# Softmax inverses and two late weights moved to GpSimd's DMA queue, in a two-layer attention kernel

## The chip, the cores and the metric

The kernel runs on one core of one Trainium2 chip. The metric is the device time of one execution in microseconds, taken as the median of several runs. Everything is float32.

## What is computed

The reference applies two layers to an image batch `x` of shape (8, 32, 32, 512).

```
# layer 0: group norm, 8-head self-attention over 1024 tokens, residual
xn  = group_norm(x) * gn_scale + gn_bias                 # 32 groups of 16 channels
qkv = xn @ w_qkv + b_qkv
out = softmax(q k^T / 64) v                              # per image, 8 heads of 64
x   = x + out @ w_out + b_out

# layer 1: deformable attention over 256 sampled keys, per image
q_img   = layernorm(x) @ wq + bq
o       = gelu(depthwise_conv_7x7_stride2(q_img) + dw_b)
offsets = tanh(o @ pw_w)                                 # 16 x 16 points
smp     = bilinear_samples(x, reference_points + offsets)
kv      = smp @ wv + bv
att     = softmax((x @ mq_w + mq_b)(kv @ mk_w + mk_b)^T) (kv @ mv_w + mv_b)
z       = att @ mo_w + mo_b + x
out     = gelu(layernorm(z) @ mlp_w + mlp_b) + z
```

## The kernel before

The kernel makes two passes. The **first pass** (about 0 to 2130 us) is layer 0, with the depthwise convolution of the images that are already done woven into it. The **second pass** is the rest of layer 1. The instructions of every engine run in the order in which the program issues them (`InOrder`), so each engine, and each engine's DMA queue, is a strict line. All of the pass's instructions are issued through one helper, which is why the profile puts nearly all of them on line 54.

The first pass is a row of 256 **units**. A unit is one tile of 128 queries for one pair of heads; an image has 4 pairs times 8 tiles, 32 units (`per`). In a unit, `MovedAttention.push` (lines 206 to 220)

- has TensorE compute two tiles of scores `sc` (one for each head, 128 by 1024),
- has VectorE take their negated maxima `nmax`, and ScalarE the exponentials `e` with their row sums,
- has VectorE transpose `e` in blocks of 32 into `sq`.

After every second unit, `moved` (lines 222 to 231) issues 16 DMAs `et<-sq` of 128 KB on SyncE's queue, which complete the transpose. TensorE multiplies `et` by the values about two units later (`part`, tile `av`). A **block** is four units: four query tiles of one head pair, which share one `av` tile.

When a block's four tiles of sums are complete, `share` (lines 170 to 180) has VectorE take their reciprocals and transpose them into `rsT`; a DMA stores `rsT` in DRAM as `rs_d`. `spread` (lines 182 to 191) reads it back with two DMAs `inv<-rs_d`, each of which hands one head's inverses to 64 partitions. `scale` (line 193) multiplies `av` by `inv` into `attT`.

All other work is put into **places**. `at(place, step)` notes a step for a place counted in units; `run_due` runs the noted steps in order of place, those below n + 0.8 between the exponentials and the transposes of unit n, and those below n + 1 after them. So a place decides where in each engine's line a step's instructions stand. The places that the change and the prediction touch are these:

- `attention_out` (lines 767 to 785): for a block whose last unit is m, n = m + 3. `share` is at n - 1.9, `spread` at n - 1.1 (for the last three blocks of the pass n - 0.3), the scaling at n + 1.85. SyncE's queue carries the store and both reads; for the last three blocks it is GpSimd's queue.
- `conv_chunk` (lines 919 to 966): the depthwise convolution runs in units 26 to 56 of the plan, by taps. For one kind of tap ScalarE multiplies into one of two buffers `part_x` and GpSimd adds it to `oa`; the other kind VectorE does alone. A unit's taps stand at 0.05 and 0.9.
- `out_steps` (lines 708 to 765): for each of an image's 8 output tiles GpSimd fetches `xr`, adds a bias row, and later multiplies and adds the normalized tile `hat`; SyncE's queue stores `mid` (the residual sum) and `hat_d`. The convolution's operand comes from `hat_d`.
- `load_weight` (line 540): GpSimd's queue loads a whole weight (1 MB) into the single tile `w`: `w_out` at 0.95 and 9.95, `wq` at 7.6 and 15.6 of an image.
- `fold_steps` (lines 800 to 878): in the last image, weights of layer 1 are multiplied with one another beforehand. It loads `wv` (at 17.7) and `mk_w` (19.3) whole by GpSimd; `w_out` (25.2 and on, four quarters, 0.5 units apart) and `mv_w` (27.2 and on, four quarters, 0.7 apart) come by ScalarE's queue. Tile `raw` shares its three buffers with the normalized input `xT`.

The second pass calls `share` and `spread` too, on SyncE's queue (lines 1401 and 1405).

Of the kernel before, what the change touches and what calls it, by code (L numbers as in the profile page):

```python
# [9 lines left out]
F32 = mybir.dt.float32  # L10
# [7 lines left out]
P = 128  # L18
B = 8
H = W = 32  # L20
S = H * W
C = 512
NC = C // P
NT = S // P
# [42 lines left out]
class Attention:  # L67
# [99 lines left out]
                    stop=(j == nkt - 1),  # L167
                )

    def share(self, sums, queue=None):  # L170

        nc = self.nc
        self.queue = queue or nc.sync
        rs = self.shares[self.turns % 2]
        self.turns += 1
        nc.vector.reciprocal(rs[:, 0 : 2 * NQT], sums.rearrange("p h i -> p (h i)"))
        turned = self.work.tile([P, SQ], F32, tag="rsT", name="rsT", bufs=2)
        nc.vector.transpose(turned, rs)
        self.share_d = self.dram.tile([P, SQ], F32, tag="rs_d", name="rs_d", bufs=3)
        self.queue.dma_start(self.share_d, turned)  # L180

    def spread(self):

        inv = self.work.tile([P, NSQ, NQT, SQ], F32, tag="inv", name="inv", bufs=self.n_inv)
        there = self.share_d.rearrange("(r c) q -> r (c q)", r=NSQ)
        for h in range(2):
            self.queue.dma_start(
                inv[ds(h * HD, HD)].rearrange("p r i q -> p r (i q)"),
                there[:, ts(h, NQT * SQ)].partition_broadcast(HD),
            )  # L190
        return inv
# [57 lines left out]
def attention_then_deformable_attention(  # L249
# [30 lines left out]
    nc = tc.nc  # L280
# [20 lines left out]
    def by_chunk(w):  # L301
        return w.rearrange("(c p) o -> p c o", p=P)
# [65 lines left out]
    def at(place, step):  # L368
        due.append((place, len(due), step))
# [140 lines left out]
    with ExitStack() as l0:  # L510
# [3 lines left out]
        nc = InOrder(tc)  # L514
# [23 lines left out]
        room_w = {}  # L538
# [3 lines left out]
            room_w["w"] = work.tile([P, NC, C], F32, tag="w", name="w", bufs=1)  # L542
            nc.gpsimd.dma_start(room_w["w"], by_chunk(w))

        def load_quarter(w, c):
            if c == 0:
                room_w["w"] = work.tile([P, NC, C], F32, tag="w", name="w", bufs=1)
            nc.scalar.dma_start(room_w["w"][:, c, :], by_chunk(w)[:, c, :])

        lng_row = load_row(wp, ln_g, "lng_row")  # L550
        lnb_row = load_row(wp, ln_b, "lnb_row")

# [214 lines left out]
        def attention_out(attT, hp, qt, n, et, sums, values):  # L767

            blk, t = divmod(qt, NQT)
            half = t // 2  # L770
            for first in (True, False):
                at(n + 1.02 - first, lambda first=first: att.part(et, values, hp, half, first))
            if half == 0:
                return

            share = {}

            def scale():
                t = attT[hp, blk] = work.tile([P, QB], F32, tag="attT", name="attT", bufs=NQB * NHP)
                att.scale(t, share["inv"])  # L780

            last = n > B * per - NT
            at(n - 1.9, lambda: att.share(sums, nc.gpsimd if last else nc.sync))
            at(n - (0.3 if last else 1.1), lambda: share.update(inv=att.spread()))
            at(n + 1.85, scale)

        def last_places(n, t):
# [12 lines left out]
        def fold_steps(first):  # L800

            raws, wT = {}, {}

            rows = {}

            def row(name, dst, raw, vec):
                rows[name] = ByRow(dst, raws[raw], vec)

            def spare():
                return work.tile([P, NC, QB], F32, tag="xT", name="raw", bufs=NX_T)  # L810

            def fetch(name, w):
                raws[name] = spare()
                nc.gpsimd.dma_start(raws[name], by_chunk(w))

            def turn(name, m):
                if name == "v" and m == 0:
                    wT[name] = spare()
                src = room_w["w"] if name == "v" else raws["wq"]
                ps = mm_tile()  # L820
                for c in range(NC):
                    nc.tensor.transpose(ps[:, ts(c, P)], src[:, c, ts(m, P)], ident)
                nc.scalar.copy(wT[name][:, m, :], ps)

            def product(dst, tag, name, raw, i):
                if i == 0:
                    fold[dst] = kept(tag)
                ps = project(lambda m: wT[name][:, m, ts(i, P)], lambda m: raws[raw][:, m, :])
                nc.scalar.copy(fold[dst][:, i, :], ps)

            at(first + 18.3, number)
            for part in range(4):
                at(first + 18.35 + part, lambda part=part: load_biases(part))
            at(first + 19.3, set_refs)
            at(first + 17.7, lambda: load_weight(wv))
            at(first + 19.3, lambda: fetch("mk", mk_w))
            for m in range(NC):
                at(first + 23.5 + m // 2 + 0.05 * (m % 2), lambda m=m: turn("v", m))
            def quarter(name, w, c):
                if c == 0:  # L840
                    raws[name] = spare()
                nc.scalar.dma_start(raws[name][:, c, :], by_chunk(w)[:, c, :])

            for c in range(NC):
                at(first + 25.2 + 0.5 * c, lambda c=c: load_quarter(w_out, c))
                at(first + 27.2 + 0.7 * c, lambda c=c: quarter("mv", mv_w, c))
                at(first + per + 1.24 + 0.001 * c, lambda c=c: quarter("wq", wq, c))
            for i, place in enumerate((25.5, 27.5, 28.5, 29.5)):
                at(first + place, lambda i=i: product("wvk", "wC", "v", "mk", i))
            def row_tile():  # L850
                return work.tile([P, C], F32, tag="v", name="row_b", bufs=5)

            def col_tile():
                return work.tile([P, NC], F32, tag="mu", name="col", bufs=2)

            at(first + 24.65, lambda: row("k", bvk, "mk", bv_c))
            at(first + 24.651, lambda: rows["k"].away(row_tile(), nc.gpsimd))
            at(first + 27.9, lambda: rows["k"].back(col_tile(), nc.gpsimd))
            raws["wq"] = None

            for i, place in enumerate((30.5, 31.5, 32.5, 32.52)):
                at(first + place, lambda i=i: product("wvv", "wB", "v", "mv", i))
            last = first + per
            at(last + 0.6, lambda: wT.update(q=spare()))
            at(last + 2.41, lambda: rows["k"].add(nc.vector))
            at(last + 3.5, lambda: row("v", bvv, "mv", bv_c))
            at(last + 3.51, lambda: rows["v"].away(row_tile(), nc.scalar))
            at(last + 4.28, lambda: rows["v"].back(col_tile(), nc.scalar))
            at(last + 3.6, lambda: fetch("mq", mq_w))
            for m in range(NC):  # L870
                at(last + 4.27 + 0.001 * m, lambda m=m: turn("q", m))
            for i in range(NC):
                at(last + 4.5 + 0.01 * i, lambda i=i: product("wqq", "wA", "q", "mq", i))
            at(last + 4.48, lambda: row("q", bqq, "mq", bq_c))
            at(last + 4.481, lambda: rows["q"].away(row_tile(), nc.scalar))
            at(last + 4.515, lambda: rows["q"].back(col_tile(), nc.scalar))
            for name in ("v", "q"):
                at(last + 4.9, lambda name=name: rows[name].add(nc.vector))
# [208 lines left out]
    with ExitStack() as l1:  # L1087
# [297 lines left out]
        def unit_steps(n):  # L1385
            hi, hp = divmod(n, NHP)
            b = hi // 2
            u = dict(tiles=NQT, at=0, v=lambda j, h: vals[b][:, j, ds((2 * hp + h) * HD, HD)])

            def scores():  # L1390
                u["q"], u["k"] = queries.pop((hi, hp)), keys[b][:, hp, :]
                u["e"] = att.scores(u)

            def scale():
                if hp == 0:
                    attH[hi] = work.tile([P, NHP, QB], F32, tag="attH", name="attH")
                att.scale(attH[hi][:, hp, :], u["inv"])

            at(n, scores)
            at(n + 0.02, lambda: att.moved(u, 0))  # L1400
            at(n + 0.039, lambda: att.share(u["sums"]))
            at(n + 0.04, lambda: att.moved(u, 1))
            at(n + 0.0401, lambda: att.taken(u, 0))
            at(n + 0.041, lambda: att.taken(u, 1))
            at(n + 0.0411, lambda: u.update(inv=att.spread()))
            last = n + 1 == 2 * B * NHP
            at(n + (1.3 if last else 1.1), lambda: att.product(u))
            at(n + (1.305 if last else 1.2), scale)
            if not last and n:
                at(n + 0.042, lambda: query_step(*divmod(n + 1, NHP)))  # L1410
# [135 lines left out]
```

## Time and profile before

| what | value |
|---|---|
| median of 3 runs | 3262.32 us (3259.76 to 3265.22) |
| the profiled execution | 3264.03 us, span 3262.3 us |
| mean granted TensorE clock | 0.998 |
| instructions | 59564 |
| data moved by DMA | 674.31 MB, mean 207 GB/s |
| DMA time, share of 16 engines: SyncE's queue (q1) | 56.8% |
| the same: GpSimd's (q0) | 13.7% |
| the same: ScalarE's (q10) | 0.4% |

The profile comes from one execution. Times are counted from the first instruction of the span. PE is TensorE's matmul, PEld its weight load, DVE is VectorE, ACT is ScalarE, POOL is GpSimd, SP is SyncE; a q behind a name means the engine's instruction queue. A row of a waits view reads: who waited, for whom, in total, how often, the longest. A row of a timeline reads: start, duration, engine, operation, and in brackets the idle time before it and what ended it. The page leaves out instructions that issue DMAs when it counts busy time.

### The profile page before, as it was taken

The page shows a single profiled execution, that of the slowest core. Times are in us where ns is not written, and L with a number is a line of the kernel's source. Part 1 is how long each engine was busy: PE and PEld are TensorE (multiplying, and loading weights), DVE is VectorE, ACT ScalarE, POOL GpSimd, SP SyncE. Part 2 cuts the span into 40 slices and gives each one's busy share as a digit, 9 for nine tenths or more (in the row PEclk, how much of TensorE's full clock was granted, in tenths as well). Part 3 has the DMA queues.
Part 4 walks back from the last instruction along what each step waited for, and adds up shares of the span by engine and source line. Part 5 has one row for each costly group of instructions (what it writes and reads, how often), then busy time and mean ns, then how long its engine had stood idle before and what let it go on. Part 6 is the DMA issues. An engine that isn't in the chain of part 4 may idle for free.

```text
span 3262.3 us, 59564 instructions
## 1 busy us (share of the span) xinstructions
PE 3217.9 (99%) x21588; PEld 1301.2 (40%) x21588; DVE 2522.9 (77%) x3457; ACT 1780.8 (55%) x3826; POOL 1593.5 (49%) x2026
## 2 busy tenths in 40 slices
PE   8999999999999999999999999999999999999999
PEld 4444344344344444444444434333333333333333
DVE  5776778898888888788788888557868787676765
ACT  3443356566567567557657656335555555554442
POOL 1001316755764665664674577225556565653323
PEclk9999999999999999999999999999999999999999
DMA  5666766777677766676676677678777786887873
GB/s 171 169 179 162 210 181 180 211 200 186 204 196 191 203 197 177 204 211 178 181 223 183 177 216 211 180 228 272 219 240 242 228 264 211 264 259 229 265 236 130
DMA packets 479325, 674.31 MB, mean 207 GB/s; under 512 B 76828, under 2 KB 268632, under 8 KB 478776
## 3 DMA queue, kind: packets, MB, share of 16 engines
q1 hardware_dynamic: 434528, 529.53, 56.8%
q0 software_dynamic: 41136, 136.78, 13.7%
q10 hardware_dynamic: 3368, 4.20, 0.4%
q8 instruction: 171, 2.80, 0.4%
q14 instruction: 122, 1.00, 0.1%
HBM read 263.17 MB, written 138.69 MB: 123 GB/s over the span
## 4 chain that ended last, share of the span: by engine, by line
PE 89%; DVE 3%; ACT 2%; DMA 2%; POOL 1%; issue 1%; SPq 1%; POOLq 0%; DVEq 0%; ACTq 0%
PE mm L54 55%; PE sc L54 17%; PE av L54 17%; ACT e L54 1%; DVE nmax L54 1%; SPq L54 1%; DMA et<-sq_d 1%; DVE sq L54 1%; POOL oa L54 0%; DVE chunk L54 0%; DMA w<-in_L_conv_w_out_dram 0%; DMA sq_d<-sq 0%; POOL xr L54 0%; DMA row<-mid,ii 0%; ACT part_x L54 0%
## 5 line engine op out<-in xcount | busy, mean ns | idle before, releaser
L54 ACT ACTIVATE e<-sc,nmax 128x1024 f32<-128x1024 f32 (+1 forms) x1024 | 803.0, 797 | 531.4 <-DVE nmax L54 524.7
L54 DVE TENSOR_REDUCE nmax<-sc 128x1 f32<-128x1024 f32 (+1 forms) x640 | 750.2, 1212 | 291.3 <-PE sc L54 286.0
L54 POOL TENSOR_TENSOR oa<-part_x,oa 128x256 f32<-128x256 f32 x852 | 639.4, 751 | 542.5 <-ACT part_x L54 496.4
L54 DVE STREAM_TRANSPOSE sq<-e 128x1024 f32<-128x1024 f32 x640 | 764.3, 1225 | 118.5 <-ACT e L54 97.7
L54 ACT ACTIVATE part_x<-pad_x,dww_x 128x256 f32<-128x256 f32 x852 | 441.2, 545 | 259.9 <-POOL oa L54 258.4
L54 PE MATMUL sc<-k,q 64*64 64x512 f32 x4096 | 512.3, 603 | 8.8 <-ACT e L54 6.7
L54 PE MATMUL av<-et,v 128*64 128x256 f32 x4096 | 499.2, 386 | 11.7 <-DMA et<-sq 4.5
L54 PEld LDWEIGHTS av<-et,v 128*64 128x64 f32 x4096 | 273.7, 137 | 328.8 <-issue 162.1
L54 POOL TENSOR_TENSOR mv<-mv,minus_half 128x1 f32<-128x1 f32 x128 | 76.3, 596 | 389.0 <-DVE mv L54 388.0
L54 PEld LDWEIGHTS sc<-k,q 64*64 64x64 f32 x4096 | 137.5, 132 | 314.6 <-issue 208.4
L54 POOL TENSOR_TENSOR chunk<-parts,chunk 128x256 f32<-128x256 f32 x240 | 185.3, 772 | 137.2 <-ACT parts L54 123.2
L54 DVE SCALAR_TENSOR_TENSOR od<-pad_x,dww_x,od 128x256 f32<-128x256 f32 x276 | 232.7, 843 | 5.5
L54 PE MATMUL mm<-wo,attH 128*64 128x512 f32 x1024 | 233.7, 598 | 0.0
L54 PE MATMUL mm<-wC,xT 128*64 128x256 f32 x2048 | 232.1, 379 | 0.0
L54 PE MATMUL mm<-xT,wB 128*64 128x512 f32 x1024 | 230.7, 592 | 0.6 <-DVE xT L54 0.6
L54 PE MATMUL mm<-hat_h,wA 128*64 128x512 f32 x1024 | 230.9, 593 | 0.0
L54 PE MATMUL mm<-xT,wA 128*64 128x512 f32 x1024 | 230.7, 592 | 0.0
L54 PE MATMUL mm<-w,attT 128*64 128x512 f32 x1024 | 230.1, 592 | 0.3 <-DMA w<-in_L_conv_w_out_dram 0.3
L54 PE MATMUL mm<-wm,zT 128*64 128x512 f32 x976 | 220.7, 592 | 0.5 <-ACT zT L54 0.5
L54 ACT ACTIVATION_READ_ACCUMULATOR e<-sc,nmax 128x1 f32 x1024 | 209.1, 204 | 0.0
L54 PEld LDWEIGHTS mm<-wC,xT 128*64 128x64 f32 x2048 | 148.0, 137 | 77.7 <-issue 6.4
L54 PE MATMUL mm<-w,hat_x 128*64 128x512 f32 x768 | 170.2, 593 | 0.0
(198 smaller groups left out, 3457.6 us busy)
## 6 DMA issues: line engine op xcount, KB each, us to landing
et<-sq SPq DMA_DIRECT2D x2048, 128.0 KB
sq_d<-sq SPq DMA_DIRECT2D x128, 512.0 KB
et<-sq_d SPq DMA_DIRECT2D x128, 512.0 KB
inv<-rs_d SPq DMA_DIRECT2D x250, 128.0 KB
xr<-mid POOLq DMA_DIRECT2D x64, 256.0 KB
xr<-in_x_dram POOLq DMA_DIRECT2D x62, 256.0 KB
x<-in_x_dram POOLq DMA_DIRECT2D x60, 256.0 KB
out_dram<-res POOLq DMA_DIRECT2D x60, 256.0 KB
```

The lines of the kernel that those rows point to most:

```text
L54: return self.tc.keep_in_program_order(op(*args, **kwargs))
```

## The change

In the first pass, all blocks now use GpSimd's queue for the store of `rsT` and the two reads of the inverses, not just the last three. VectorE's part stays at n - 1.9. The store becomes a step of its own at n - 1.17, and the reads stand at n - 0.3 for all blocks. (For the last three blocks the queue and the reads' place are as before, and only the store moves, from n - 1.9 to n - 1.17.) In the last image, `w_out` and `mv_w` are loaded whole by GpSimd's queue at 25.2 and 27.2 instead of in quarters by ScalarE's. The quarters of `wq` at the end of the pass stay on ScalarE's queue. The second pass issues the same as before, through a step `shared`.

```diff
-    def share(self, sums, queue=None):
+    def share(self, sums):
         nc = self.nc
-        self.queue = queue or nc.sync
         rs = self.shares[self.turns % 2]
         self.turns += 1
         nc.vector.reciprocal(rs[:, 0 : 2 * NQT], sums.rearrange("p h i -> p (h i)"))
         turned = self.work.tile([P, SQ], F32, tag="rsT", name="rsT", bufs=2)
         nc.vector.transpose(turned, rs)
         self.share_d = self.dram.tile([P, SQ], F32, tag="rs_d", name="rs_d", bufs=3)
-        self.queue.dma_start(self.share_d, turned)
+        return turned
 
-    def spread(self):
+    def spread(self, queue):
...
         for h in range(2):
-            self.queue.dma_start(
+            queue.dma_start(
...
-        def load_quarter(w, c):
-            if c == 0:
-                room_w["w"] = work.tile([P, NC, C], F32, tag="w", name="w", bufs=1)
-            nc.scalar.dma_start(room_w["w"][:, c, :], by_chunk(w)[:, c, :])
...
-            last = n > B * per - NT
-            at(n - 1.9, lambda: att.share(sums, nc.gpsimd if last else nc.sync))
-            at(n - (0.3 if last else 1.1), lambda: share.update(inv=att.spread()))
+            at(n - 1.9, lambda: share.update(rs=att.share(sums)))
+            at(n - 1.17, lambda: nc.gpsimd.dma_start(att.share_d, share["rs"]))
+            at(n - 0.3, lambda: share.update(inv=att.spread(nc.gpsimd)))
             at(n + 1.85, scale)
...
+            at(first + 25.2, lambda: load_weight(w_out))
+            at(first + 27.2, lambda: fetch("mv", mv_w))
             for c in range(NC):
-                at(first + 25.2 + 0.5 * c, lambda c=c: load_quarter(w_out, c))
-                at(first + 27.2 + 0.7 * c, lambda c=c: quarter("mv", mv_w, c))
                 at(first + per + 1.24 + 0.001 * c, lambda c=c: quarter("wq", wq, c))
...
+            def shared(u):
+                rs = att.share(u["sums"])
+                nc.sync.dma_start(att.share_d, rs)
...
-            at(n + 0.039, lambda: att.share(u["sums"]))
+            at(n + 0.039, lambda: shared(u))
...
-            at(n + 0.0411, lambda: u.update(inv=att.spread()))
+            at(n + 0.0411, lambda: u.update(inv=att.spread(nc.sync)))
```

## The prediction

> **What bounds the kernel now.** I read the page's busy shares first, then what TensorE waited for, then what SyncE's queue waited for in the first pass (30 to 2100 us), and last the rows around single places.
>
> ```profile
> PE 3217.9 (99%) x21588; PEld 1301.2 (40%) x21588; DVE 2522.9 (77%) x3457; ACT 1780.8 (55%) x3826; POOL 1593.5 (49%) x2026
> ```
>
> TensorE is busy for 3217.9 of 3262.3 us, at a granted clock of 0.998. So no change of queues can win more than the 44 us that are left, and some 13 of those are the start (the first 100 us hold 87.2 us of work). What TensorE waited for, over the whole span:
>
> ```profile
> PE mm L54 <- DMA x<-in_x_dram: 8.4, 1, 8.4
> PE sc L54 <- ACT e L54: 7.7, 10, 1.3
> PE av L54 <- DMA et<-sq_d: 5.0, 4, 2.2
> PE av L54 <- DMA et<-sq: 4.5, 3, 2.5
> PE av L54 <- DVE rs L54: 2.7, 1, 2.7
> PE av L54 <- DVE mv L54: 1.6, 2, 1.1
> ```
>
> An `av` wait is one for the moved exponentials `et`. The releaser named is not always the last one: by the trace's DMA records the `DVE rs` row (at 2058) and the `DVE mv` rows (at 356 and 1927) end when the last of 16 `et` transfers lands. The same holds for a wait of 1.0 us at 878 that is put down to `DVE od`. So 1.1 us at 356, 1.0 at 421, 1.0 at 878, 0.5 at 1927, 2.5 at 1998 and 2.7 at 2058 are waits for `et`. In SyncE's queue:
>
> ```profile
> SPq L54 <- DVE sq L54: 251.5, 79, 31.4
> SPq L54 <- DMA rs_d<-rsT: 103.3, 55, 5.9
> SPq L54 <- POOL hat L54: 44.0, 27, 4.6
> SPq L54 <- DMA et<-sq: 35.1, 34, 2.9
> ...
> SPq L54 <- DMA raw<-in_L_conv_mv_w_dram: 5.5, 2, 4.6
> SPq L54 <- DMA w<-in_L_conv_w_out_dram: 4.8, 2, 4.4
> ```
>
> The reader is to see two things. The queue that carries `et` stands still for 103 us because an inverse may only be read once the sums' tile has landed. And it stands still, twice for over 4 us, for weights that it did not send: these are the quarters on ScalarE's queue.
>
> **What goes from SyncE.** 61 blocks lose one `rs_d` (median 0.57 us) and two `inv` (0.61 each): 61 x 1.79 = 109 us of issue, and the 103 us of waiting. Nearly all of it is hidden: most groups of 16 `et` land 1 to 9 us before TensorE wants them. It shows only where the wait above follows such a block:
>
> ```profile
> 402.83 0.41 SPq L54 DMA_DIRECT2D mid<-xr  x1
> 403.32 0.71 SPq L54 DMA_DIRECT2D rs_d<-rsT  x1
> 404.12 0.87 SPq L54 DMA_DIRECT2D hat_d<-hat  x1
> 407.13 1.27 SPq L54 DMA_DIRECT2D inv<-rs_d  x2
> 408.51 14.55 SPq L54 DMA_DIRECT2D et<-sq  x21
> ```
>
> These `et` could have gone at 405.74, when `sq` was written. They went 2.8 us later, and the last landed at 421.77, 0.1 us before TensorE's late start. Without `rs_d` and `inv` the queue is free at 405, so the 1.0 us goes. The groups that end at 356, 878 and 1927 began 2.9, 1.7 and 2.8 us late for the same reason: 1.1 + 1.0 + 0.5 go too. The one at 1998 began 0.9 us late and then waited 2.7 us for an `inv` to land; the load of `wv` is in its way as well (8.67 us to landing), so I take 1.5 of its 2.5. Sum: **5.1 us won**; bounds 2.5 (half of it is lost to hat rows that come later) and 6.1 (all five waits). In these places `av` starts when the scores end; the next late thing is the attention product's own tile, none in the rows.
>
> The Trainium skill ("DMA: Bandwidth & Descriptors", section "Issuing engines are not separate DMA queues") speaks against this part: issuing from more engines saves only the sequencer's time. By that rule this term would be 0. The rows above differ from it, since here the sequencer's wait stands in front of other transfers.
>
> **What comes to GpSimd.** The three rows of `rs_d` there took 0.56 us, the six of `inv` 0.64. A block adds 0.56 half a unit before the taps' second group and 1.28 a unit later. From unit 59 on GpSimd runs back to back at nearly all these places (gaps of 0.02 to 0.08 us before the next instruction), so what stands behind moves by 0.5 and 1.2 us. It then idles 1.6 to 2.6 us before the next unit's taps, so the delay ends within the unit. Who waits for it is ScalarE: a tap needs one of two `part_x` buffers, and the next unit's exponentials stand behind the taps in its order. For each of these places I took the ScalarE idle time ahead of the next `e` and the time from the last `e` to TensorE's next scores; what the delay exceeds is a stall. In most it is covered (for instance unit 138: 6.3 us idle; unit 142: 2.9 us to spare). It is not covered in three kinds of place:
>
> ```profile
> 1150.10 0.58 POOL L54 DMA_DIRECT2D xr<-in_x_dram  x1
> 1150.69 1.28 POOL L54 TENSOR_TENSOR hat<-hat,lng_row 128x512 f32<-128x512 f32 x1
> 1152.05 1.27 POOL L54 TENSOR_TENSOR hat<-hat,lnb_row 128x512 f32<-128x512 f32 x1
> ...
> 1154.04 0.56 ACT L54 ACTIVATE part_x<-pad_x,dww_x 128x256 f32<-128x256 f32 x1 [4.74 <-POOL oa L54]
> 1154.52 1.09 ACT L54 ACTIVATE e<-sc,nmax 128x1024 f32<-128x1024 f32 x1
> ```
>
> - Here `rs_d` goes in before `hat`, at 1150.69. ScalarE has waited 4.74 us for GpSimd, its `e` ends at 1156.70, and TensorE's scores begin at 1156.56 and already stumble (2.22 us for 1.95). The 0.55 us falls on TensorE. This is the 13th unit of an image: 0.55 in units 141 and 205, 0.5 in 173, 0.2 in 77, none in 109 and 237: 1.8 us.
> - Units 62, 94, 126, 158, 190 and 222 (the 30th): `inv` goes in among six taps, `e` has no idle time ahead and 0.85 us to spare: 1.2 - 0.85 = 0.4, six times: 2.4 us.
> - The last image, units 245 and 246: TensorE already waits for `e` there (0.68 us at 2019.01), so 0.56 + 1.28 = 1.8 us fall on it whole.
>
> Sum: **6.0 us lost**; bounds 2 (if ScalarE's two buffers take up the delays of the first two kinds) and 9 (if the 0.55 to 1.2 us spare of some 17th and 5th units go too). `hat_d` on SyncE waits for `hat`, now 0.55 us later; with `rs_d` and `inv` gone from ahead of `et` that is covered. In the first image and a half GpSimd waits anyway (a wait of 55.7 us for `x`), so nothing is added. Waits of `inv` for its own sums: 3.2 to 10 us lie between the two on GpSimd, and sums land in 2.2 to 3.4 us; behind two `x` loads some 4. I take nothing; where it is short, the next `e` has 5 us and more. The first pass's scaling is due two units (15 us) after `inv`, which lands in 4 to 6.
>
> **The last image's weights.** Eight quarters of 256 KB leave ScalarE's queue (8 x 0.34 us, ScalarE is idle there for 2.5 us before each `e`). `w_out` goes whole ahead of `part_x` and the inverses on GpSimd, at some 2042.6; `mv` goes behind two additions, and waits there for TensorE to leave `xT` at 2049.3; `bq_x` and `col`, behind it, are not wanted for 10 us. SyncE's two long waits (4.4 and 4.6 us) go. That speaks for the 2.7 us at 2058 (a row by stages; TensorE's busy time comes first, and the last three columns are the granted clock, the DMA engines' busy share and GB/s):
>
> ```profile
> 2058.00:2061.00 3.00, 0.42 (x4) 0.00 (x0) 2.49 (x4) 1.21 (x3) 0.00 (x0) 1.00 0.90 273
> ...
> 2062.40:2065.80 3.40, 3.40 (x13) 1.51 (x10) 1.32 (x2) 0.00 (x0) 2.10 (x3) 0.50 0.83 205
> ```
>
> The first row says why I don't book it: the DMA engines are 90% busy at 273 GB/s. From 2041.8 on `et` (2.1 MB), `w_out` (1.05), `o` (0.5), `part_x`, `inv` (0.26 each) and half of the `mv` that is now earlier (0.7) make 4.9 MB; at the 252 GB/s of this stretch that is 19.4 us, to 2061.2. Now the group lands at 2060.9. So the wait stays as it is: **0**, bounds -4.4 (it goes with what follows) and +4 (below, the slower rival). The second row is what follows it: the granted clock is 0.50 for 3.4 us, 1.7 us lost, so the wait costs 4.4.
>
> The Trainium skill ("TensorE: Matmul & The Clock Gate", section "HAM oscillation") puts the rule at idle gaps over about 3.4 us. By that rule this wait would cost 2.7 alone. The row (2.7 us idle, then 0.50) decides here; after the 2.5 us at 1998 the clock stayed at 1.00.
>
> **Sum.** -5.1 + 6.0 + 0 = +0.9 us. The profiled execution took 3264.0 us (span 3262.3 and 1.7 around it), 1.7 above the median of 3262.3; on the median the sum gives 3263.2, say 3263.5.
>
> **Rivals.** A measurement of this kernel can tell about 0.2%, 6.5 us, from no change: below 3255.8 is faster, above 3268.8 slower.
> - *Even* (0.46): the two sums cancel, as above; 3263.5, own range 3256 to 3269.
> - *Faster* (0.22): SyncE, no longer held by others' weights, gets `et` through at 2058 in time, and the half clock goes with the wait; GpSimd's delays are half covered. -5.1 - 4.4 + 3 = -6.5 to -8.5: 3254 to 3256. For it: 4.4 us of SyncE standing still at 2042.5 to 2047.5. Against it: the 0.90 busy share.
> - *Slower* (0.30): in the last image the inverses stand behind `o` and the whole of `w_out` in GpSimd's queue. Such a load took 6.0 to 10.9 us to land, and `o` 5.3. VectorE wants the inverses at 2056.14 and takes nothing else meanwhile, so from a landing after that on, the scores' maxima, `e` and TensorE wait. If they land at 2058 to 2060, 2 to 4 us are added to the wait for `et`. With GpSimd's 6.0 and half of the gain: +6.0 - 2.5 + 4 = +7.5: 3270.
> - *Nothing is seen* (0.02): `rs_d` and `inv` are covered on both sides; 3262, which lies within the even case.
>
> The even case and this last hold 0.48. Range 3253 to 3274: from the faster case with all five waits gone to the slower one with the upper bound of GpSimd's cost.
>
> **What would show it.** Right: SyncE's row for `rs_d` is gone from the first pass (what remains is the second's); TensorE's `et` waits at 356, 421, 878 and 1927 are gone; scores of the 13th and 30th units begin 0.4 to 0.6 us later than now; a wait of 2 to 4 us stays near 2058. Wrong, to the faster side: that wait and its half clock are gone. Wrong, to the slower side: `attT` waits for `inv`, or new stretches at half clock.

## The result, and the profile after

The changed kernel takes 3284.91 us (median of 4 runs, 3284.02 to 3286.46) against 3263.77 us for the kernel before on the same chip (3259.76 to 3265.78). The ratio is 1.0063, with a 95% interval of 1.0047 to 1.0079: it is slower by some 21 us. The prediction said 3263.5, with a range to 3274.

The profiled execution's span is 3283.3 us at a mean granted clock of 0.998. From the page after, the line of busy shares, and from what TensorE waited for:

```profile
PE 3236.0 (99%) x21588; PEld 1307.6 (40%) x21588; DVE 2517.2 (77%) x3457; ACT 1778.1 (54%) x3826; POOL 1698.6 (52%) x2211
```

```profile
PE sc L54 <- ACT e L54: 12.5, 17, 1.9
...
PE av L54 <- DMA et<-sq: 5.5, 3, 3.9
```

TensorE's instructions are the same, yet its busy time grew by 18.1 us: scores that stand still between their matmuls count as busy (the page's row for `sc` alone rose from 512.3 to 529.9 us). Its waits for `e` rose from 7.7 to 12.5 us. GpSimd's busy time rose by 105.1 us with 185 instructions more: 61 x 3 DMA issues and the two weights', 0.57 us each. So the page counts GpSimd's DMA issues as busy, unlike those of the other engines. The chain that ended last, before and after:

```profile
PE 89%; DVE 3%; ACT 2%; DMA 2%; POOL 1%; issue 1%; SPq 1%; POOLq 0%; DVEq 0%; ACTq 0%
PE 76%; POOL 6%; ACT 6%; DMA 5%; DVE 4%; issue 2%; SPq 1%; POOLq 0%; ACTq 0%; DVEq 0%
```

GpSimd and ScalarE gained most (1% to 6%, and 2% to 6%), but transfers gained too (2% to 5%), so the chain alone does not tell what the time went to. SyncE's queue in the first pass (30 to 2100 us) has no row for `rs_d` any more, and waits for its real source instead, 461.9 us where it was 251.5:

```profile
SPq L54 <- DVE sq L54: 461.9, 119, 31.4
SPq L54 <- POOL hat L54: 66.7, 26, 5.1
```

Where the time goes is best seen by the start of each unit's scores, this kernel minus the kernel before, from the two traces (us; units count from 0, image b starts at unit 32 b; "end" is the end of the span). The rows below `after` are the experiments of the next section. Each row comes from one execution, and a single wait that another execution does not have can move a row by 4 to 7 us from there on (see the last section); so the steps from unit to unit that come back in several images say more than a row's end.

| kernel | unit 0 | 64 | 128 | 224 | 248 | 253 | end |
|---|---|---|---|---|---|---|---|
| after | -0.6 | -2.0 | 2.1 | 11.9 | 16.8 | 18.0 | 21.0 |
| e1_quarters | -1.2 | -2.6 | 2.0 | 11.7 | 17.1 | 18.7 | 20.6 |
| e8_none | -0.6 | -2.9 | -3.1 | -3.2 | -3.1 | -0.8 | -1.1 |
| e3_dummy | 0.0 | -0.3 | 4.2 | 9.4 | 12.6 | 10.5 | 11.5 |
| e5_store | -0.6 | -4.2 | -3.0 | 1.3 | 3.6 | 4.8 | 5.4 |
| e6_reads | 0.3 | -3.0 | 1.6 | 6.5 | 14.3 | 15.4 | 18.4 |
| e4_ahead | -1.0 | -1.5 | -2.2 | -2.4 | -2.5 | -1.4 | -0.4 |
| e10_one | -1.5 | -0.8 | 1.1 | 7.1 | 11.2 | 12.8 | 17.6 |

The changed kernel first wins some 3 us (units 26, 45 and 53), then loses 2 us at the end of image 1, 2 to 4 in each of the images 2 to 6, and 6 in the last. In images 4 to 6 these losses come back each time: 0.55 us at units 143, 175 and 207 (unit 15 of an image), 1.0 us at 145, 177 and 209 (unit 17), 0.3 at 151, 183 and 215 (unit 23), and 0.6 at 160, 192 and 224 (unit 0 of the next). Image 4 alone loses another 0.95 at 152. Units 15 and 0 lie behind places that the prediction named; units 17, 23 and 24 do not.

### The profile page after: what moved, and what is told of

It reads as the page before. It is cut to its first block, busy times and chain, and to the rows that moved or that the text cites. A ratio compares the mean times of both kernels' runs of the same rounds, so it can differ in the third digit from the quotient of the medians.

```text
span 3283.3 us, 59533 instructions
## 1 busy us (share of the span) xinstructions
PE 3236.0 (99%) x21588; PEld 1307.6 (40%) x21588; DVE 2517.2 (77%) x3457; ACT 1778.1 (54%) x3826; POOL 1698.6 (52%) x2211
## 4 chain that ended last, share of the span: by engine, by line
PE 76%; POOL 6%; ACT 6%; DMA 5%; DVE 4%; issue 2%; SPq 1%; POOLq 0%; ACTq 0%; DVEq 0%
PE mm L54 47%; PE sc L54 15%; PE av L54 14%; ACT e L54 3%; POOL oa L54 2%; DMA et<-sq 1%; POOL hat L54 1%; ACT part_x L54 1%; DVE sq L54 1%; SPq L54 1%; DMA et<-sq_d 1%; POOL xr L54 1%; DVE nmax L54 1%; DMA sq_d<-sq 1%; DVE chunk L54 1%
## 5 line engine op out<-in xcount | busy, mean ns | idle before, releaser
L54 PE MATMUL sc<-k,q 64*64 64x512 f32 x4096 | 529.9, 603 | 14.6 <-ACT e L54 11.5
```

What stands on the lines that cost most here:

```text
L54: return self.tc.keep_in_program_order(op(*args, **kwargs))
```

## The experiments

Each ran in 5 rounds beside the kernel before; the ratio is against that. The theory at the start: GpSimd's added time stands in a ring (`e`, `part_x`, `oa`, the next `e`) that has no slack, so it reaches TensorE. The rivals: the late weights, or transfers that land late.

**Which half of the change.** e1_quarters puts the last image's weights back; e2_whole makes only that part of the change.

```diff
 # e1_quarters, against the changed kernel (e2_whole: the reverse, against the kernel before)
-            at(first + 25.2, lambda: load_weight(w_out))
-            at(first + 27.2, lambda: fetch("mv", mv_w))
             for c in range(NC):
+                at(first + 25.2 + 0.5 * c, lambda c=c: load_quarter(w_out, c))
+                at(first + 27.2 + 0.7 * c, lambda c=c: quarter("mv", mv_w, c))
```

> The changed kernel, but the last image's w_out and mv_w come in quarters by ScalarE's queue again. Theory (GpSimd's time): the loss comes from the 0.56 + 1.28 us of GpSimd's time for each block, which travel from unit to unit round the ring of e, part_x, oa and the next e; the two weights carry only 0 to 4 of the 21 us, so this kernel takes 17 to 21 us more than the one before (3281 to 3285). Rival (the weights): they carry 10 us or more, so this kernel is at most 11 us above the one before.

> The kernel before, with only the last image's two weights whole by GpSimd's queue. Theory (GpSimd's time): 0 to 4 us more than the kernel before. Rival (the weights): 10 us or more.

e1_quarters: 3284.67 us against 3264.02, ratio 1.0064 (1.0050 to 1.0078). e2_whole: 3265.58, ratio 1.0005 (0.9996 to 1.0014). The weights carry nothing that can be told from zero; the whole loss is in the inverses.

**GpSimd's time alone.**

```diff
 # e3_dummy, against the kernel before (SyncE's queue untouched)
+            if not last:
+                at(n - 1.17, lambda: idle_work(1))   # tensor_tensor 128x1, pow
+                at(n - 0.3, lambda: idle_work(2))
```

> The kernel before with its DMAs untouched; for each block but the last three GpSimd gets idle work of the same length at the places of the changed kernel: one tensor_tensor of 128x1 (such a pow takes 0.57 to 0.60 us) at n - 1.17 and two at n - 0.3. Its results are used by nothing. Theory (GpSimd's time): the losses of the changed kernel without its gains on SyncE, which the trace puts at some 7 us: 20 to 28 us above the kernel before. Rival (transfers: the loss comes from sums and inverses that land late or stand in the way of other transfers in GpSimd's queue): 0 to 4 us above.

3273.24 us against 3264.02, ratio 1.0030 (1.0019 to 1.0040): 9 us, between theory and rival. Work that moves no data and that nobody reads costs TensorE time, so late transfers are not needed for a loss. But 11 us are missing. The trace says where: the losses at units 15 and 17 are there (0.54 and 1.03 us at 175 and 177), those at units 23 and 0 are not. Nor is the dummy quite what it stands for: between an `xr` issue and `hat` it makes VectorE's tap beside them shorter (0.48 us in 12 places; 1.8 in the kernel before, 2.34 in e1_quarters), so e3_dummy may put the price of GpSimd's time too low.

**Is it the place on GpSimd?** The same queue, the same three DMAs for each block, at places where GpSimd waits for `part_x`.

```diff
 # e4_ahead, against e1_quarters (last: the pass's last three blocks, unchanged)
-            at(n - 1.17, lambda: nc.gpsimd.dma_start(att.share_d, share["rs"]))
-            at(n - 0.3, lambda: share.update(inv=att.spread(nc.gpsimd)))
+            at(n - (1.17 if last else 0.98), lambda: nc.gpsimd.dma_start(att.share_d, share["rs"]))
+            at(n + (-0.3 if last else 0.02), lambda: share.update(inv=att.spread(nc.gpsimd)))
```

> As e1_quarters, but the store stands at n - 0.98 and the reads at n + 0.02, each right ahead of a unit's first taps, where GpSimd waits 1.6 to 2.6 us for part_x (the last three blocks keep their places). Theory (GpSimd's time on the ring): work that stands where GpSimd waits for ScalarE delays nobody, the losses go and SyncE's gains stay: 3 to 7 us below the kernel before (3257 to 3261). Rival (any GpSimd time counts, or SyncE's gains are not from these DMAs): within 3 us of e1_quarters, so 14 us or more above the kernel before.

3264.11 against 3264.02, ratio 1.0005 (0.9996 to 1.0014). A move by 0.2 to 0.3 units takes away the 20.7 us, as far as can be told. The expected gain of 3 to 7 us does not appear; e8_none says why.

**The ring, shown at one place.** In the changed kernel GpSimd's line at units 174 and 175 (part of its timeline, with the idle time before an instruction in brackets) reads:

```profile
1425.94 1.54 POOL L54 TENSOR_TENSOR oa<-part_x,oa 128x256 f32<-128x256 f32 x2 [1.67 <-ACT part_x L54]
...
1429.23 1.25 POOL L54 DMA_DIRECT2D inv<-rs_d  x2
1430.50 0.57 POOL L54 TENSOR_TENSOR mv<-mv,minus_half 128x1 f32<-128x1 f32 x1
1431.03 2.34 POOL L54 TENSOR_TENSOR oa<-part_x,oa 128x256 f32<-128x256 f32 x3
1435.04 1.53 POOL L54 TENSOR_TENSOR oa<-part_x,oa 128x256 f32<-128x256 f32 x2 [1.66 <-ACT part_x L54]
```

and in the kernel before, the same units:

```profile
1419.39 1.54 POOL L54 TENSOR_TENSOR oa<-part_x,oa 128x256 f32<-128x256 f32 x2 [1.67 <-ACT part_x L54]
...
1422.70 0.57 POOL L54 TENSOR_TENSOR mv<-mv,minus_half 128x1 f32<-128x1 f32 x1
1423.24 2.34 POOL L54 TENSOR_TENSOR oa<-part_x,oa 128x256 f32<-128x256 f32 x3
1427.24 1.54 POOL L54 TENSOR_TENSOR oa<-part_x,oa 128x256 f32<-128x256 f32 x2 [1.66 <-ACT part_x L54]
```

Read the brackets. From tap to tap a unit takes 9.10 us where it took 7.85, longer by `inv`'s 1.25, and yet GpSimd idles 1.66 us in both. The idle time did not shrink by what was put in; it moved. GpSimd waits there for ScalarE's `part_x`, ScalarE issues that behind its `e`, and `e` stands behind a tap that waits for GpSimd. ScalarE's rows in the changed kernel show the same from the other side (2.49 and 2.81 us before):

```profile
1431.79 0.53 ACT L54 ACTIVATE part_x<-pad_x,dww_x 128x256 f32<-128x256 f32 x1 [3.73 <-POOL oa L54]
...
1441.81 0.56 ACT L54 ACTIVATE part_x<-pad_x,dww_x 128x256 f32<-128x256 f32 x1 [4.05 <-POOL oa L54]
```

The delay is not yet seen by TensorE at unit 174, whose `e` has 2.9 us to spare before. It is handed on to unit 175, whose `e` had 0.1, and there it costs 1.0 us, one unit further on than the prediction looked. e10_one moves these two reads, one block's of an image's eight:

```diff
 # e10_one, against e1_quarters
+            moved = (n - 3) % per == 11
-            at(n - 0.3, lambda: share.update(inv=att.spread(nc.gpsimd)))
+            at(n + (0.02 if moved else -0.3), lambda: share.update(inv=att.spread(nc.gpsimd)))
```

> As e1_quarters, but in each image the reads of one block (last unit 11, counted from 0) stand at n + 0.02 instead of n - 0.3: 0.32 units later, ahead of the next unit's first taps, where GpSimd idles. The other seven blocks of an image are as in e1_quarters. Theory (GpSimd's time among taps travels round the ring of e, part_x and oa for several units until ScalarE idles): the 1.0 us that TensorE loses at each image's 18th unit, four units after these reads, goes six times: 4 to 6 us below e1_quarters, so 3278 to 3281. Rival (the delay ends within the unit, as the prediction had it, and the loss at the 18th unit has another cause): within 2 us of e1_quarters.

3279.17 us against 3262.77 (e1_quarters: 3284.67 against 3264.02), ratio 1.0045 (1.0032 to 1.0058): the 4 to 6 us come. Against e1_quarters the start of scores gains 0.74, 0.74, 1.02, 1.02, 1.00 and 1.01 us at units 81, 113, 145, 177, 209 and 241, 5.5 us together. Unit 176's scores, in the changed kernel and then in e10_one:

```profile
1443.52 3.04 PE L54 MATMUL sc<-k,q 64*64 64x512 f32 x16
```

```profile
1441.02 2.01 PE L54 MATMUL sc<-k,q 64*64 64x512 f32 x16
```

16 matmuls that take 1.95 us when nothing is late took 3.04: a busy row can hide a wait.

**Store and reads apart, and SyncE's gain apart.**

```diff
 # e5_store: the store as in e1_quarters, the reads on SyncE's queue
-            at(n - 0.3, lambda: share.update(inv=att.spread(nc.gpsimd)))
+            at(n - (0.3 if last else 1.1), lambda: share.update(inv=att.spread(nc.gpsimd if last else nc.sync)))
 # e6_reads: the reads as in e1_quarters, the store on SyncE's queue
-            at(n - 1.17, lambda: nc.gpsimd.dma_start(att.share_d, share["rs"]))
+            at(n - (1.17 if last else 1.9), lambda: (nc.gpsimd if last else nc.sync).dma_start(att.share_d, share["rs"]))
 # e8_none: neither (but for the last three blocks); one tile of 0.001 takes the inverses' place
```

> As e1_quarters, but only the store rs_d goes by GpSimd's queue, at n - 1.17; the two reads are on SyncE's queue again, at n - 1.1. (The last three blocks stay as in e1_quarters.) In e1_quarters VectorE's tap od, which takes 0.48 us alone, takes 1.24 us in 13 places where rs_d is issued beside it and an addition follows; with dummy work instead of the store it takes 0.48. Theory (the store's place: it delays GpSimd's ring and lengthens VectorE's tap): the store carries most of the loss, some 2 us per image, and SyncE still waits for sums to land, so 6 to 13 us above the kernel before. Rival (length of work: 1.28 of the 1.84 us per block are the reads): at most 4 us above.

> As e1_quarters, but only the two reads inv go by GpSimd's queue, at n - 0.3; the store stays on SyncE's queue at n - 1.9. (The last three blocks stay as in e1_quarters.) Theory (the store's place): up to 1 us lost per image, and SyncE's waits for landed sums are gone as well: 4 us below to 5 us above the kernel before. Rival (length of work): 8 us or more above.

> As e1_quarters, but for all blocks but the last three there are no stores and no reads at all: the scaling uses one tile filled with 0.001, so the first pass's softmax is not divided by its sums. VectorE's part stays. What SyncE alone wins, without GpSimd's cost. By the prediction's first step: 5.1 us below the kernel before (2.5 to 6.1), so 3258 to 3262. By the trace's lag of e4_ahead (2 us at the end of the first pass): 2 us. Rival (issue slots are all that is saved, and they are covered): 0.

e5_store: 3271.18 against 3262.85, ratio 1.0018 (1.0010 to 1.0027). e6_reads: 3282.96, ratio 1.0052 (1.0038 to 1.0066). e8_none: 3262.66, ratio 0.9993 (0.9983 to 1.0003). e5_store lies where the theory had it (6 to 13 us), e6_reads does not: the theory that the store carries most of the loss fell. With the reads put to e5_store it becomes e1_quarters and loses 12 to 15 us more, so the reads carry most. But e6_reads does not show their length alone: its sums land late, behind SyncE's transfers, and by the waits of GpSimd's queue from 440 to 2130 us it stood still for 36.4 us in 17 places ahead of `inv` until `rs_d` had landed (e1_quarters: 1.3 us, once). And SyncE's gain alone is 0 to 2 us at the end, though it is 4.6 us at unit 245. It is given back at units 246 and 247 (0.8 us each, `e` is late there with or without the change) and at 253, where TensorE now comes to its wait for `et` earlier:

```profile
2059.24 3.68 PE L54 MATMUL av<-et,v 128*64 128x256 f32 x16 [3.91 <-DMA et<-sq]
```

This is e8_none; before it was 2.69 us, at 2061.11.

**Why a store costs more than work of its length.** In e3_dummy, at unit 189, VectorE's taps and what GpSimd did beside the third of them:

```profile
1545.48 2.20 DVE L54 SCALAR_TENSOR_TENSOR od<-pad_x,dww_x,od 128x256 f32<-128x256 f32 x3
...
1546.84 0.73 POOL L54 TENSOR_TENSOR one<-one,minus_half 128x1 f32<-128x1 f32 x1
```

The same in e1_quarters:

```profile
1545.92 2.99 DVE L54 SCALAR_TENSOR_TENSOR od<-pad_x,dww_x,od 128x256 f32<-128x256 f32 x3
...
1547.27 0.58 POOL L54 DMA_DIRECT2D rs_d<-rsT  x1
1547.87 2.44 POOL L54 TENSOR_TENSOR oa<-part_x,oa 128x256 f32<-128x256 f32 x3
```

Three taps take 2.20 us beside the dummy and 2.99 beside the store; by the trace it is the third, 0.48 against 1.27. It begins while `rs_d` is issued, and it ends 0.29 us after the addition behind `rs_d`. The maxima, `e` and the scores stand behind it. At unit 23 this is the loss: e5_store, with the store alone, has the same 0.3 us there. At unit 0 it is half of the cause. e5_store has the same long taps ahead of it (1.28 us at 1540, for instance) and loses nothing, e6_reads loses 0.2 us in each of five images, and only store and reads together lose 0.6. Over the whole of e1_quarters, 13 taps begin beside an `rs_d`, and they take 1.24 us on average; beside the dummy 13 take 0.48.

```diff
 # e9_twin, against e3_dummy: a second store of the same sums, which nobody reads
-                at(n - 1.17, lambda: idle_work(1))
+                at(n - 1.17, lambda: nc.gpsimd.dma_start(
+                    dram.tile([P, SQ], F32, tag="rs_2", name="rs_2", bufs=3), share["rs"]))
 # e16_behind, against e5_store: behind the unit's last taps
-            at(n - 1.17, lambda: nc.gpsimd.dma_start(att.share_d, share["rs"]))
-            at(n - (0.3 if last else 1.1), lambda: share.update(inv=att.spread(nc.gpsimd if last else nc.sync)))
+            at(n - (1.17 if last else 1.02), lambda: nc.gpsimd.dma_start(att.share_d, share["rs"]))
+            at(n - (0.3 if last else 0.95), lambda: share.update(inv=att.spread(nc.gpsimd if last else nc.sync)))
```

> As e3_dummy, with the 128x1 dummy at n - 1.17 replaced by a second store of the same sums to a scratch tensor by GpSimd's queue (0.56 us, as long as the dummy); nothing reads it, and SyncE's queue is untouched. Theory (a DMA that GpSimd issues lengthens VectorE's tap beside it, work of the same length doesn't): the losses of 0.6 us before an image's first scores and 0.3 us at its 23rd, absent in e3_dummy, come back: 4 to 8 us more than e3_dummy, so 13 to 17 us above the kernel before. Rival (only GpSimd's time counts, and what e3_dummy lacks against e1_quarters is the reads' or sums' landing): equal to e3_dummy within 2 us, 7 to 11 us above.

> As e5_store (only the store by GpSimd's queue), but the store stands at n - 1.02 instead of n - 1.17 and the reads on SyncE's queue at n - 0.95 instead of n - 1.1: 0.15 units later, behind the unit's last taps instead of ahead of their second half. Theory (place: behind the taps no od of VectorE begins beside the store, and GpSimd idles next): the 6 to 8 us of e5_store go, 0 to 2 us above the kernel before. Rival (SyncE's reads, now later in its line, or GpSimd's 0.56 us wherever it stands): 5 us or more above.

e9_twin: 3283.25 us against 3262.85, ratio 1.0051 (1.0036 to 1.0065). Its medians give 20 us, its ratio 17, which is 7 to 11 us over e3_dummy; the theory said 13 to 17, and 4 to 8. The losses at units 23 and 0 (0.3 and 0.7 us) are back, and 13 taps take 1.25 us. By the two traces units 0, 23 and 24 make 5.4 us of the difference. Another 5.3 us are steps at units 141 and 173, where `av` starts late (after waits of 1.34 us at 1148.66 and 2.18 us at 1415.25, the second with a half clock behind it). It also starts late at one of these two units in e2_whole, e14_wlast, e17_best and e18_spread, whose GpSimd places differ, so these steps are not put down to the store. e16_behind: 3266.28 against 3263.30, ratio 1.0006 (0.9997 to 1.0015), where e5_store had 1.0018; no tap begins beside a store. The median is 1 us over what was expected, the interval holds it.

**Images and versions.** e11_images leaves the last image's blocks as before; e13_reads stores on SyncE's queue and reads at n + 0.02 on GpSimd's; e12_later and e17_best move w_out's quarters behind the group of `et` that TensorE waits for.

```diff
 # e11_images, against e1_quarters: last image as in the kernel before
+            if n > B * per - per: ...
 # e13_reads, against e6_reads
-            at(n - 0.3, lambda: share.update(inv=att.spread(nc.gpsimd)))
+            at(n + (-0.3 if last else 0.02), lambda: share.update(inv=att.spread(nc.gpsimd)))
 # e12_later, against e4_ahead; e17_best, the same against e13_reads
-                at(first + 25.2 + 0.5 * c, lambda c=c: load_quarter(w_out, c))
+                at(first + 28.5 + 0.5 * c, lambda c=c: load_quarter(w_out, c))
 # e14_wlast, against e13_reads: w_out whole by GpSimd's queue at 30.9
 # e15_both, against e14_wlast: mv_w whole by GpSimd's queue at 28.2
 # e18_spread, against e13_reads: w_out's quarters by GpSimd's queue at 28.5 + 0.8 * c
```

> As e1_quarters, but the last image's blocks keep the queue and the places of the kernel before. Theory: what was lost up to the last image stays (10 to 14 us by the trace's lag), and the last image's 7 us go: 3273 to 3278. Rival (half or more of the loss is made in the last image, where ScalarE's e already bounds TensorE): 3264 to 3271.

> As e6_reads (store on SyncE's queue at n - 1.899, reads by GpSimd's), but the reads stand at n + 0.02, where GpSimd waits for part_x. Theory (place on GpSimd decides): the 17 to 20 us of e6_reads go, 0 to 4 us below the kernel before. Rival (reads on GpSimd's queue cost time wherever they stand): 8 us or more above.

e11_images: 3278.97 against 3262.77, ratio 1.0058 (1.0044 to 1.0071), 1 us over its range: by the ratio some 2, by the medians 4 us of the loss are the last image's. e13_reads: 3261.69, ratio 0.9996 (0.9987 to 1.0005). Again place decides: 21 us less than e6_reads by the medians, each against the kernel before, 18 by the ratios.

> As e4_ahead, and the last image's w_out comes in its four quarters at 28.5 to 30 instead of 25.2 to 26.7, behind the et that TensorE waits for at 2058 (it is wanted at 33.1). Theory (that wait is for the DMA engines' bytes): 1.05 MB less ahead of it at 250 GB/s are 4 us; the 2.3 to 4 us of waiting and the half clock behind it go: 2 to 5 us below e4_ahead. Rival (the wait is for SyncE's order or for something else): equal to e4_ahead within 2 us.

> As e13_reads, and the last image's w_out comes whole by GpSimd's queue at 30.9 (it is wanted at 33.1) instead of in quarters by ScalarE's at 25.2 to 26.7; mv_w stays in quarters by ScalarE's. In e12_later the wait of 4 us at 2055 went when w_out's quarters stood later, and a wait of 3.2 us came at 2070, where SyncE's et stands behind a quarter that it did not send. Theory (bytes ahead of et decide the wait, and quarters that share SyncE's semaphores hold the next group): the wait at 2058 and its half clock go, and what comes at 2070 is at most 2 us: 2 to 5 us below e13_reads, 3257 to 3260. Rival (the wait only moves to a later group): within 2 us of e13_reads.

> As e14_wlast, and mv_w whole by GpSimd's queue at 28.2 (it is wanted at 30.5), so that ScalarE's queue carries no weight until 33.2. Theory: SyncE's et waits for nobody else's weights, 0 to 2 us below e14_wlast, 3256 to 3260. Rival (the bytes alone count; the megabyte is in the way of the group at 2070): 1 to 3 us above e14_wlast.

> As e13_reads, with the last image's w_out in quarters by ScalarE's queue at 28.5 to 30, as in e12_later. The two best edits together, as a candidate that may beat both kernels. Theory: e13_reads's 1 us and the 2.5 us that e12_later won over e4_ahead add up: 3259 to 3261, 2 to 4 us below the kernel before. Rival (the wait at 2058 only moves to the group after it, as in e14_wlast): within 2 us of the kernel before.

> As e13_reads, with the last image's w_out in quarters by GpSimd's queue, 0.8 units apart from 28.5 to 30.9: later than e13_reads, thinly spread, and on a queue that shares no semaphores with SyncE's. Theory (both bytes ahead of et and shared semaphores hold the groups at 2058 and 2070): at least as good as e17_best, 3257 to 3261. Rival (the bytes have to go somewhere in these 30 us, and the wait moves): within 2 us of the kernel before.

e12_later: 3261.66 against 3262.77, ratio 1.0000 (0.9991 to 1.0009): 1.2 us below e4_ahead by the medians, 1.6 by the ratios, where 2 to 5 were expected. The wait before unit 253 is gone (5.7 us by the lag against e4_ahead), and one of 3.2 comes at the next group:

```profile
2073.28 1.95 PE L54 MATMUL av<-et,v 128*64 128x256 f32 x16 [3.18 <-DMA et<-sq]
```

e14_wlast: 3264.52 against 3263.30, ratio 1.0001 (0.9992 to 1.0010); e15_both: 3264.96, ratio 1.0008 (0.9999 to 1.0017). The late wait is 3.95 and 3.35 us. In all these traces the DMAs of SyncE and ScalarE report on the same eight semaphores, GpSimd's on eight others. In e14_wlast SyncE still waits for `mv_w`'s quarters (7.1 us in three waits), in e15_both for no weight any more, and the wait for `et` stays: the shared semaphores are not what makes it. Both kernels miss their expectation. e17_best: 3262.97 against 3266.55, ratio 0.9987 (0.9978 to 0.9997), and e18_spread: 3266.06, ratio 0.9997 (0.9987 to 1.0007). So e17_best is 0.13% below the kernel before, and the interval just leaves out no change. It is the lowest ratio of 17 experiments, its late wait is still there (2.63 us), and 0.13% is less than the 0.2% that the prediction took as the least that can be told: a gain over the kernel before is not shown. e18_spread misses its expectation.

## Why the prediction was wrong

**"What comes to GpSimd", 6.0 us lost, is the step that failed.** e1_quarters against e8_none, both against the kernel before, puts it at 21 us (20.7 and -0.2), over twice its upper bound of 9 (by the ratios 23). The sentence that failed is "It then idles 1.6 to 2.6 us before the next unit's taps, so the delay ends within the unit". The idle time is the ring's own waiting. I checked each place's slack for the same unit and its next scores, and found 2.9 us to spare where the delay was then handed on. By kinds, from the lag of e1_quarters:

- Unit 15 of an image (the prediction's "13th unit" is its cause): 1.8 us booked, 4.1 measured in images 2 to 7. It is 0.55 us where the rows said 0.55, and 0.8 in images 2, 3 and 7, where I had read 0.2 or nothing; 0.3 of each 0.8 is there in e8_none too.
- Unit 17: nothing booked, 6.2 us in six images. e10_one shows the mechanism, and 5.5 of the 6.2 us go with it; e8_none has 0.6 of them without GpSimd's part.
- Unit 0 (the prediction's "30th unit"): 2.4 booked, 5.1 measured: 0.6 in each of units 96, 128, 160, 192 and 224, and 2.0 at 63 and 64. The place was right, and half of the cause: `inv` among the taps. The other half is the lengthened tap of VectorE, which I did not look at. (The dummy has no loss at these units, e5_store none, e6_reads 0.2 at 96 to 224, e9_twin 0.7 at each.)
- Unit 23 in images 4 to 6: nothing booked, 1.0 measured, by the same tap. Unit 24 in image 4: nothing booked, 0.9 measured. Ahead of it GpSimd's queue stood still for 1.19 us between the two reads of `inv` (at 1230.64), as it did for 1.36 us ahead of unit 63 (and in two more places, where no loss followed); the trace names nothing that it waited for, and the cause stays open. Unit 16 in images 2 and 3: nothing booked, 1.0 measured.
- The last image: 1.8 booked, and 7.0 us between units 224 and 253, of which e8_none has 2.4 without GpSimd's part. A part that the sum did not hold at all is the clock: behind a wait of 1.92 us for `e` the granted clock was 0.54 from 2034.6 to 2038.0 in the changed kernel, where it was 1.00 before, and unit 248 starts 1.3 us later (e3_dummy, with a wait of 1.84 us there and no half clock, loses nothing at 248). In the changed kernel these scores read:

```profile
2034.58 4.30 PE L54 MATMUL sc<-k,q 64*64 64x512 f32 x16 [1.92 <-ACT e L54]
```

**"What goes from SyncE", 5.1 us won.** Each place was right: in e8_none the units behind the waits at 356, 421, 878 and 1927 gain 1.13, 1.05, 1.05 and 0.56 us (booked: 1.1, 1.0, 1.0 and 0.5), and the one behind 1998 gains 1.6 (booked: 1.5). What failed is what came next: "none in the rows" was late next, I wrote. But 1.9 us went back in small steps at units 79, 81, 111, 113, 239 and 242, `e` was late at units 246 and 247, and the wait at 2058 took the rest. e8_none puts the sum at 0 to 2 us. The Trainium skill's rule ("DMA: Bandwidth & Descriptors", section "Issuing engines are not separate DMA queues"), which would have made this term 0, came nearer to the end time than my sum, though the five waits did shrink.

**The last image's weights, 0, were right** (e2_whole: 1.6 us, which cannot be told from zero). The wait stayed, 3.27 us there, with SyncE's two stalls gone. Bytes in the way explain it better than the order of the queue: it goes when 1.05 MB are moved behind it, and comes back at the next group. No run moved the bytes alone, so this is argued, not shown.

**The signs and the rivals.** The four signs that the prediction listed for itself came true: `rs_d`'s row is gone, so are the four waits for `et`, the two kinds of place lose 0.55 and 0.6 us (seen two units on, at the scores of units 15 and 0), and a wait of 3.86 us stays in the last image (at 2075 now). But so did one of the two signs against it, to the slower side: the new stretch at half clock at 2035. A list of places that come true is no proof of a sum; what fails is a place that is not on the list. The slower rival had the right side and the wrong mechanism: it put the loss behind `o` and `w_out` in the last image, and without the whole weights nothing changes (e1_quarters).

## What to carry to other kernels

Idle time of an engine ahead of work that it gets from another engine is not slack when that other engine waits for the first one in turn: follow a delay round the ring until a unit where a member idles for an outside reason, and book it at the first unit on the way that has none to spare. Put a queue's DMA issues where the engine already waits (in this kernel 61 blocks' issues cost nothing that can be told from zero ahead of the taps, and some 20 us among them), and take a saved stall as won only up to the next wait that does not depend on it. A group's busy time can hide waits: compare the length of 16 matmuls with what they take undisturbed.

## What the runs showed of the hardware

- A VectorE tap (`od`, 128x256, two inputs in SBUF) takes 0.44 to 0.48 us when GpSimd is idle, 0.83 beside GpSimd's `oa`, and 0.48 beside its 128x1 dummy. When it begins beside a DMA issue of GpSimd and takes over 1 us, it ends 0.3 us after the first computing instruction behind the issue or issues, in the kernel before and after alike: 1.26 us with `rs_d` and `oa`, 1.8 with `xr` and `hat`, 2.34 with `xr`, `rs_d` and `hat`. The Trainium skill ("SBUF — State Buffer", section "Who interferes with whom") has a VectorE instruction with two SBUF inputs contend with a GpSimd instruction that reads SBUF; the 0.83 agrees. That a DMA issue makes VectorE wait for the instruction behind it as well is seen in these rows; why was not tried.
- The half clock does not follow from the length of the idle time alone. After 2.69 us without work the granted clock was 0.50 for 3.4 us in the kernel before (at 2062), and after 1.92 us it was 0.54 for as long in the changed kernel (at 2035); but after 2.63 us in e17_best it stayed at 1.00, and after 3.18 us in e12_later the next 16 matmuls took their usual 1.95. What it depends on besides was not tried.
- The same instructions can differ from run to run by single waits. In e13_reads unit 173 starts without one; in e14_wlast, which issues the same up to 2000 us, a wait of 3.30 us at 1398 ahead of `av`, with a half clock behind it, makes the unit 4.7 us later. e17_best and e18_spread have the same wait at the same unit (3.46 and 3.64 us). So the medians of 5 rounds, not one trace, carry the verdicts of a few us.
